# Last stage of a four-layer graph network kernel: five groups keep y and x in SBUF, six groups start together, zero rows and first fetches are issued earlier

## The chip, the cores and the metric

The kernel runs on one core of a Trainium2 chip. The metric is the time of the program on the device in microseconds (us), taken as the median of several executions. Lower is better. The engines are named as the profile names them: PE is the matrix engine (PEld its weight load), DVE the vector engine, ACT the scalar engine, POOL the GpSimd engine, SP the engine that here only issues DMAs.

## The reference, cut to what matters

There are 128 batches, each with 128 nodes of 128 features (`x`, float32) and a 128 x 128 matrix of edges (`adj`, int32). Four layers follow each other, and each has the form

```
h = relu(layernorm(x));  x = x + layer(h, adj)
```

- Layer 0 averages the neighbours by relation, adds a projection of the node itself, and applies a layer norm and a relu.
- Layer 1 takes D = |h_i - h_j| for every pair of nodes, projects it to 64 channels, and normalises each channel over all batches and pairs. A leaky relu and a second projection turn that into one score per pair. The softmax of the scores (edges only) weighs the neighbours. The weighed rows are projected, giving `y`, normalised per channel over all batches and nodes, passed through a leaky relu, and projected together with `h`.
- Layers 2 and 3 are graph attention with four heads and with one: e_ij = leaky(a_i + a_j), softmax over the edges, weighed sum of the projected rows. Layer 3 ends with an elu.

The two normalisations over all batches in layer 1 are what cut the kernel into stages: nothing behind one of them can start before every batch is through.

## The kernel before, in words

A group is four batches (`G = 4`), so there are 32 groups (`NG`). The kernel has three long stages.

**First stage.** Layer 0 of each group, and the first projection of the pair differences of each batch. The projected pairs of a batch, 2 MB, are stored in DRAM (`HP`, line 368). The orders of all engines come from `_ordered`, a list planner with written costs. It starts with a search for the largest relation number (`part`, `top`, `flag`), whose result decides a branch (line 627). In these inputs the branch that is taken only fills the DRAM array of neighbour sums with a constant (line 676, two DMAs of 1.5 MB and 6 MB). Small loads of weights (lines 197, 204, 713 to 728) stand in SP's queue around that branch, where the framework's scheduler has put them; the load of group 3's `x` and `adj` (lines 416, 417) stands behind them.

**Middle stage.** It runs over slots of one batch each. `fetch` reads half a batch of `HP` (1 MB) into one of `FETCHED = 10` buffers (line 841). ACT, DVE and PE turn the halves into scores, which are written to DRAM rows along a diagonal (line 924) and read back as a square (`u`, line 931). A chain of steps per group, spread over the slots, does the softmax, the weighing and the projections. Its `stored` step writes the group's new `x` to DRAM (line 978, array `X`) and its `y` (line 980, array `Z`), except that the last `KEPT = 8` groups keep `y` in SBUF. The step of group g falls in slot 4g + 16. The cells of the DRAM rows that the diagonal leaves free must be zero. Before the slots start, the kernel sets a tile `zero` on DVE (line 808), and writes it to both row arrays (line 811). In the program this set-up, and some small DVE and PE steps, stand ahead of the first ten fetches.

**Last stage.** Layers 2 and 3, group by group, under `tc.manual_schedule()`. `attention(g)` lists the steps of a group (loads `lz` and `lx`, mask `off`, `y`, `yl`, `po`, `x1`, then two attention layers with `mv`, `rs`, `h`, `pt`, `hT`, `pr`, `v`, `sp`, `pe`, `left`, `right`, `ps`, `e`, `w`, and at the end `ex`, `x3`, `x4`, `out`). `_planned` puts them in one order for each engine. It is a list planner with the cost written beside each step; a group may start at its due time,

```
start = max([free[engine], (n - FIRST) * period] + [done[a] + HOP for a in after])
```

so that with `FIRST = 4` and `PERIOD = 12.5` five groups are due at time zero, and one more every 12.5. Only the order is used on the chip; the times are not. Groups with `y` on chip come first. `BUFS` gives the buffers of each tile, and `ONE`, `TWO` the PSUM banks (four single, two double).

An alternative last stage (behind line 1378) runs when the scores could overflow, and is not taken here.

Of the kernel before, what the change touches and what calls it, by code (L numbers as in the profile page):

```python
# [9 lines left out]
F32 = mybir.dt.float32  # L10
# [4 lines left out]
OP = mybir.AluOpType  # L15
AX = mybir.AxisListType

P = 128
G = 4
# [9 lines left out]
KC = 8  # L29
ROW = P + 2 * KH  # L30
# [3 lines left out]
PARTS = 16  # L34
FETCHED = 10
NT = KH // KC
KEPT = 8


ONE, TWO = 4, 2  # L40
PERIOD, FIRST, HOP, LANDING = 12.5, 4, 0.2, 3.0
HOP1 = 0.4
TINY = 2.0 ** -100
BUFS = {"y": 5, "x": 11, "off": 10, "st": 7, "mv2": 4, "rs2": 3, "nb2": 3, "h": 7, "hT2": 3, "v2": 3, "wr2": 6,
        "left2": 4, "right2": 4, "e0": 2, "e1": 3, "e2": 3, "e3": 2, "sums2": 2, "o2": 2, "mv3": 2, "rs3": 2,
        "nb3": 2, "hT3": 2, "v3": 2, "wr3": 4, "left3": 2, "right3": 2, "e": 2, "sums3": 2, "o3": 2, "ex": 2}


def _bcast(src, n):
# [30 lines left out]
def _planned(groups, period, banks):  # L80

    free, done = dict.fromkeys(("SP", "Pool", "ACT", "DVE", "PE"), 0.0), {}
    left = {tag: [0.0] * n for tag, n in banks.items()}
    tag = lambda name: "2" if name[0] == "2" else "1"
    waiting = [list(steps) for steps in groups]
    plan = []
    while any(waiting):
        best = None  # L90
        for n, steps in enumerate(waiting):
            for i, (name, engine, cost, after, takes, last, work) in enumerate(steps):
                if any(a not in done for a in after):
# [75 lines left out]
def tile_gnn_stack(ctx: ExitStack, tc: tile.TileContext, a: dict, out: bass.AP):  # L169
    nc = tc.nc  # L170
    NB = a["x"].shape[0]
    NG = NB // G
# [22 lines left out]
    def load(name, shape, src, pool=const):  # L195
        t = pool.tile(shape, F32, name=name)
        nc.sync.dma_start(t, src)
        return t
# [9 lines left out]
    dr = ctx.enter_context(tc.tile_pool(name="dr", bufs=1, space=bass.MemoryType.DRAM))  # L208
# [2 lines left out]


    HP = [dr.tile([P, NT, KC * P], F32, tag=f"hp{b}", name=f"hp{b}") for b in range(NB)]
    M8 = [res.tile([P, G, P], U8, tag=f"m{g}", name=f"m{g}") for g in range(NG)]
    MV1 = res.tile([P, NG, G, 2], F32, name="MV1")
    RS1 = res.tile([P, NG, G], F32, name="RS1")
# [42 lines left out]
    with tc.tile_pool(name="c0", bufs=1) as c0, tc.tile_pool(name="p0", bufs=2) as p0, ExitStack() as ctx0:  # L259
# [33 lines left out]
        def step(name, engine, cost, after, rank, work, takes=(), gives=()):  # L293
            steps.append((name, engine, cost, after, takes, gives, rank, work))
# [237 lines left out]
        found, n_part = {}, P * P // PARTS  # L532
        flat = a["adj"].rearrange("b t s -> b (t s)").rearrange("b (c n) -> c b n", c=PARTS)
        tops = search.tile([P, 2, PARTS // 2], F32, name="tops")
        less_1 = search.tile([P, 1], F32, name="less_1")
        nc.gpsimd.memset(less_1, -1.0)
        flag = const.tile([1, 1], I32, name="flag")
# [46 lines left out]
        w1T2 = c0.tile([P, 64], F32, name="w1T2")  # L584
        both_t = c0.tile([P, 2, KC, P], F32, name="both_t")

        def both_tokens():
            turns = search.tile([P, 2, P], F32, name="turns")
            nc.vector.tensor_scalar(w1T2, w1T, 2.0, None, op0=OP.mult)
            nc.vector.tensor_copy(turns, ident[:, None, :].to_broadcast([P, 2, P]))  # L590
            ahead = turns[:, 0, 1 + KC * BY_MAX:]
            ahead = bass.AP(tensor=ahead.tensor, offset=ahead.offset,
                            ap=[list(ahead.ap[0]), [KH, 2], [1, KC], [1, P]])
            nc.vector.tensor_tensor(both_t, ahead, ident[:, None, None, :].to_broadcast([P, 2, KC, P]), OP.add)
# [17 lines left out]
        step("flag", "DVE", 0.4, ["ptop"], -99, flagged, gives=("sm",))  # L612
        step("both_t", "DVE", 2.6, ["selfb"], 99, both_tokens)
        step("fold", "Pool", 0.5, [], 99, folds)
        for g in range(AHEAD):
            chain(g, selfb)

# [156 lines left out]
    early.close()  # L774
    middle = ctx.enter_context(ExitStack())
    keep = ctx.enter_context(tc.tile_pool(name="keep", bufs=1))
    Y = {g: keep.tile([P, G, P], F32, name=f"y{g}") for g in range(NG - KEPT, NG)}
    psum = middle.enter_context(tc.tile_pool(name="psum2", bufs=1, space=bass.MemoryType.PSUM))
    banks = {"ps": 3, "pk": 2, "sm": 3}
    with tc.tile_pool(name="c1", bufs=1) as c1, tc.tile_pool(name="p1", bufs=2) as p1:  # L780

        z0 = c1.tile([P, 1], F32, name="z0")
        nc.vector.scalar_tensor_tensor(z0, bias1, 0.01, bias1, op0=OP.mult, op1=OP.max)
# [19 lines left out]
                                       add_k[:, :, 4:8], op0=OP.mult, op1=OP.add)  # L803


        slots = []
        zero = c1.tile([P, G, ROW], F32, name="zero")
        nc.vector.memset(zero, 0.0)
        for n in range(2):
            rows = dr.tile([G, P, ROW], F32, tag=f"rows{n}", name=f"rows{n}")  # L810
            nc.sync.dma_start(rows.rearrange("g i r -> i g r"), zero)
            slots.append(rows)

        sk = []
        for n in range(2):
            t = c1.tile([P, G, 1 + 2 * KH], F32, name=f"sk{n}")
# [14 lines left out]
        def now(slot, place):  # L831
            for work in jobs.pop((slot, place), ()):
                work()

        fetched, prepared, scored = [], {}, {}

        def fetch(n):

            if n < 2 * NB:
                z = p1.tile([P, NT // 2 * KC * P], F32, name="z", bufs=FETCHED)  # L840
                nc.sync.dma_start(z, HP[n // 2][:, n % 2 * NT // 2:(n % 2 + 1) * NT // 2, :]
                                  .rearrange("p a b -> p (a b)"))
                fetched.append(z)

        def products(ps, parts, j0):
            for i, (w, v) in enumerate(parts):
# [56 lines left out]
        def chain(g):  # L903

            rows = slots[g % 2]
# [27 lines left out]
            def normed():  # L933
                t["h"] = pre_norm(p1, t["x"], MV1[:, g], RS1[:, g])
                t["cap"] = p1.tile([P, G, P], F32, name="cap")
                nc.gpsimd.tensor_scalar(t["cap"], M8[g], BIG, NEG12, op0=OP.mult, op1=OP.add)
                t["x1"] = p1.tile([P, G, P], F32, name="x1", bufs=3)
                nc.gpsimd.tensor_tensor(t["x1"], t["x"], over_group(bt), OP.add)  # L938

            def folded():  # L940
# [34 lines left out]

            def stored():
                nc.vector.bn_stats(ST2[:, g, :], t["y"].rearrange("p a b -> p (a b)"))
                nc.sync.dma_start(X[g], t["x1"])
                if g not in Y:
                    nc.sync.dma_start(Z[g], t["y"])  # L980

            at(s0 - 4, "s", to_rows)
# [116 lines left out]
        with tc.manual_schedule():  # L1099
            for g in range(NG):  # L1100
                chain(g)
            brief()
            for n in range(FETCHED):
                fetch(n)
            for b in range(-1, NB + 3 * G + 1):
                slot(b)

# [12 lines left out]
    with tc.If(nc.values_load(bounded, min_val=0, max_val=1) > 0) as cmp, \  # L1120
# [10 lines left out]
        def attention(g):  # L1131
# [4 lines left out]
            def step(name, engine, cost, after, work, takes=(), last=()):  # L1136
                steps.append(((g, name), engine, cost, [(g, n) for n in after], takes, last, work))
# [15 lines left out]
            def load(name, src):  # L1153
                nc.sync.dma_start(sb(name, [P, G, P]), src)

            on_chip = g in Y
            if on_chip:
                t["y"] = Y[g]
            else:
                step("lz", "SP", 0.4, (), lambda: load("y", Z[g]))  # L1160
            step("lx", "SP", 0.4, (), lambda: load("x", X[g]))

            def masked():
                nc.gpsimd.tensor_scalar(sb("off", [P, G, P], BF16), M8[g], 0.0, None, op0=OP.is_equal)

            step("off", "Pool", 1.5, ("lx",), masked)
            step("y", "ACT", 0.75, () if on_chip else ("lz",), lambda: nc.scalar.activation(
                t["y"], t["y"], AF.Identity, bias=bias2, scale=scale2[:, 0:1]))
            step("yl", "DVE", 0.65, ("y",), lambda: nc.vector.scalar_tensor_tensor(
# [2 lines left out]
            def rest():  # L1172
                po = bank("po")
                for k in range(G):
                    nc.tensor.matmul(po[:, k, :], t["y"][:, k, :], wtyT, start=True, stop=True)

            step("po", "PE", 0.9, ("yl",), rest, takes=("po",))
            step("x1", "DVE", 0.6, ("po", "lx"), lambda: nc.vector.tensor_tensor(t["x"], t["x"], t["po"], OP.add),
                 last=("po",))

            def layer(n, heads, wx, first):
# [194 lines left out]
            return steps  # L1376

        with tc.manual_schedule():
            for work in _planned([attention(g) for g in sorted(range(NG), key=lambda g: g not in Y)], PERIOD, {"1": ONE, "2": TWO}):
                work()  # L1380


    with cmp.Else(), tc.tile_pool(name="c2", bufs=1) as c2, tc.tile_pool(name="p2", bufs=5) as p2, \
# [83 lines left out]
        def group(g):  # L1467
            zT = Y[g] if g in Y else p2.tile([P, G, P], F32, name="zT")
            if g not in Y:
                nc.sync.dma_start(zT, Z[g])  # L1470
            x = p2.tile([P, G, P], F32, name="x", bufs=6)
            nc.sync.dma_start(x, X[g])
            yT = p2.tile([P, G, P], F32, name="yT")
            nc.scalar.activation(yT, zT, AF.Identity, bias=bias2, scale=scale2[:, 0:1])
            nc.vector.scalar_tensor_tensor(yT, yT, 0.01, yT, op0=OP.mult, op1=OP.max)
# [121 lines left out]
```

## Time and profile before

| | |
|---|---|
| median of three executions | 2812.61 us (2811.74 to 2816.77) |
| the profiled execution | 2813.74 us |
| its span, first to last instruction | 2811.9 us |
| mean granted PE clock | 0.961 |
| busy: PE, DVE, ACT, POOL | 2466.4, 2472.0, 2392.2, 1723.5 us |
| first stage | to about 1528 us |
| middle stage | about 1533 to 2336 us |
| last stage | about 2336 to 2812 us |

Share of busy time is an average over three stages that have different limits, so each stage is read for itself. The rows of digits in the page give the stages at a glance: each digit is the busy tenths of one fortieth of the span, some 70 us. A row of the timeline gives the start and duration of an instruction, and in brackets the idle time of its engine before it and what ended it. SPq is the queue of DMA issues; "to landing" is the time from an issue until the data have arrived.

### The profile page before, as it was taken

Reading aid. Unit: us, or ns where it says so; the run is one execution under the profiler, and the core shown is the slowest. Engines: PE = TensorE matmul, PEld = TensorE weight load, DVE = VectorE, ACT = ScalarE, POOL = GpSimd, SP = SyncE. Lnnn points to the kernel's source line nnn. Section 1 sums busy time; section 2 is a strip of 40 time slices with the busy share of each in tenths; the row PEclk is TensorE's granted clock in tenths of the full one; section 3 lists DMA queues with packets and bytes.
Section 4 is the critical chain, followed back from the end, with each engine's and each line's share of the span. In section 5 each row is a group of like instructions: output and inputs, shape, how many; then the busy total and the mean of one; then the engine's idle time right before and its main releaser. Section 6 shows DMA issues by size and latency. Waiting matters only on the chain.

```text
span 2811.9 us, 41767 instructions
## 1 busy us (share of the span) xinstructions
PE 2466.4 (88%) x14521; PEld 1190.8 (42%) x14521; DVE 2472.0 (88%) x4713; ACT 2392.2 (85%) x2837; POOL 1723.5 (61%) x1628
## 2 busy tenths in 40 slices
PE   3899999999999999999997798998888887998897
PEld 2333333333333333333332344444444445777775
DVE  4899999999999999999997588888888886988786
ACT  4899999999999999999997787788888755988886
POOL 6799999999999999999985000111000115655552
PEclk7999999999999999999998899999999997999998
DMA  7454555455555545555546999999999961111110
GB/s 272 172 212 202 203 214 210 199 206 205 214 206 213 210 199 206 210 213 210 206 187 240 417 410 412 413 413 412 412 412 413 409 223 42 57 61 58 61 35 28
DMA packets 180379, 653.45 MB, mean 232 GB/s; under 512 B 31028, under 2 KB 98743, under 8 KB 130999
## 3 DMA queue, kind: packets, MB, share of 16 engines
q1 hardware_dynamic: 179712, 650.44, 58.5%
q8 instruction: 120, 1.97, 0.3%
q14 instruction: 109, 0.88, 0.1%
q10 hardware_dynamic: 438, 0.17, 0.0%
HBM read 337.75 MB, written 312.80 MB: 231 GB/s over the span
## 4 chain that ended last, share of the span: by engine, by line
ACT 34%; PE 25%; DVE 21%; DMA 7%; issue 7%; POOL 5%; SPq 0%; ACTq 0%; DVEq 0%; POOLq 0%
ACT d L350 14%; ACT hs L333 10%; PE hp L319 6%; PE ps L849 6%; DVE z L892 4%; DVE d L309 3%; PE hp L322 2%; PE pv L1319 2%; DMA z<-hp 2%; POOL d L309 2%; PE pk L856 2%; DMA rows<-sk 2%; ACT o L450 1%; ACT h L491 1%; ACT hn L450 1%
## 5 line engine op out<-in xcount | busy, mean ns | idle before, releaser
L309 POOL TENSOR_TENSOR d<-xe 128x2048 f32<-128x2048 f32 x256 | 1074.4, 4202 | 60.5 <-PE hp L319 55.0
L319 PE MATMUL hp<-d,w1T 128*64 128x512 f32 x4096 | 997.5, 602 | 120.3 <-ACT hs L333 84.4
L350 ACT ACTIVATE d<-d 128x2048 f32<-128x2048 f32 x384 | 734.4, 1934 | 38.5 <-DVE d L309 20.0
L309 DVE TENSOR_TENSOR d<-xe,xp 128x2048 f32<-128x2048 f32 x256 | 579.5, 2264 | 6.9 <-PE hp L319 3.5
L319 PEld LDWEIGHTS hp<-d,w1T 128*64 128x64 f32 x4096 | 285.8, 137 | 638.9 <-issue 479.2
L333 ACT COPY hs<-hp 128x1024 f32<-128x1024 f32 x512 | 516.4, 1028 | 31.1 <-PE hp L322 25.2
L938 POOL TENSOR_TENSOR x<-x,bt 128x512 f32<-128x512 f32 x32 | 44.9, 1402 | 689.3 <-DMA x<-x 626.1
L340 DVE BATCH_NORM_STATS2 st<-hs 128x6 f32<-128x512 f32 x512 | 349.3, 682 | 42.1 <-ACT hs L333 41.7
L341 DVE BATCH_NORM_STATS2 st<-hs 128x6 f32<-128x512 f32 (+1 forms) x512 | 329.3, 643 | 0.0
L892 DVE SCALAR_TENSOR_TENSOR z<-z 128x2048 f32<-128x2048 f32 x128 | 294.5, 2301 | 21.8 <-ACT z L874 21.8
L874 ACT ACTIVATE z<-z,bias,scale 128x2048 f32<-128x2048 f32 x128 | 267.2, 2088 | 18.2 <-DMA z<-hp 17.8
L878 ACT ACTIVATE zr<-z,bias,scale 128x2048 f32<-128x2048 f32 x128 | 267.3, 2088 | 9.2 <-DMA z<-hp 7.9
L322 PE MATMUL hp<-both_t,xw 128*64 128x512 f32 x1024 | 268.0, 595 | 0.0
L849 PE MATMUL ps<-z,w2z 128*32 128x512 f32 x1024 | 144.3, 636 | 79.1 <-DVE z L892 79.1
L856 PEld LDWEIGHTS pk<-pick,su 128*128 128x128 f32 x1024 | 128.0, 196 | 131.7 <-DVE su L870 85.0
L1319 PE MATMUL pv<-wr,e 128*128 128x128 f32 x1024 | 148.0, 293 | 10.7 <-DVE e L1296 6.2
L856 PE MATMUL pk<-pick,su 128*128 128x16 f32 x1024 | 140.5, 269 | 15.8 <-DVE su L870 15.8
L849 PE MATMUL ps<-z,w2l 128*32 128x512 f32 x1024 | 141.9, 624 | 0.3 <-DMA z<-hp 0.3
L1319 PEld LDWEIGHTS pv<-wr,e 128*128 128x128 f32 x1024 | 133.5, 204 | 19.3 <-issue 3.6
L849 PE MATMUL ps<-zr,w2r 128*32 128x512 f32 x1024 | 140.8, 622 | 0.4 <-ACT zr L878 0.4
L322 PEld LDWEIGHTS hp<-both_t,xw 128*64 128x64 f32 x1024 | 80.7, 138 | 141.2 <-issue 141.2
L1296 DVE SCALAR_TENSOR_TENSOR e<-e,ps 128x512 f32<-128x512 f32 x160 | 106.8, 678 | 28.7 <-ACT ps L1293 28.0
(243 smaller groups left out, 3837.4 us busy)
## 6 DMA issues: line engine op xcount, KB each, us to landing
hp<-hs SPq DMA_DIRECT2D x128, 2048.0 KB, 6.7
z<-hp SPq DMA_DIRECT2D x256, 1024.0 KB, 14.2
x<-x SPq DMA_DIRECT2D x128, 256.0 KB, 11.6
u<-rows SPq DMA_DIRECT2D x32, 384.0 KB, 11.5
x<-in_x_dram SPq DMA_DIRECT2D x32, 256.0 KB, 3.0
adj<-in_adj_dram SPq DMA_DIRECT2D x32, 256.0 KB, 3.3
part<-in_adj_dram SPq DMA_DIRECT2D x16, 512.0 KB, 7.6
out_dram<-x SPq DMA_DIRECT2D x32, 256.0 KB, 2.5
```

Source lines behind the costliest of these rows:

```text
L309: eng.tensor_tensor(d, ahead, x[:, None, None, :].to_broadcast([P, 2, KC, P]), OP.max if t == BY_MAX else OP.subtract)
L319: nc.tensor.matmul(hp[64 * hh:64 * hh + 64, c:c + 512], w1T2 if by_max else w1T, d[:, hh, c:c + 512], start=True, stop=not by_max, skip_gr ...
L322: nc.tensor.matmul(hp[64 * hh:64 * hh + 64, c:c + 512], XW[i // NT // 2][:, i // NT % 2, :], both_t.rearrange("p h k i -> p h (k i)")[:, h ...
L333: nc.scalar.copy(halves[b][:, t, :], linear.pop(i))
L340: nc.vector.bn_stats(st[:, 2 * t, :], hs[:, 0:512])
L341: nc.vector.bn_stats(st[:, 2 * t + 1, :], hs[:, 512:1024 - P * last])
L350: nc.scalar.activation(diffs[i], diffs[i], AF.Abs)
L849: nc.tensor.matmul(ps[32 * c:32 * c + 32, :], w[:, w0:w0 + 32], v[:, 512 * c:512 * c + 512], start=j0 == 0, stop=w is w2r, skip_group_chec ...
L856: nc.tensor.matmul(pk[:, kk, 0:16], su[:, kk, :], pick.rearrange("p h j -> p (h j)"), start=True, stop=True)
L878: nc.scalar.activation(zr, z1, AF.Relu, bias=bias1, scale=scale1[:, 0:1])
L892: nc.vector.scalar_tensor_tensor(z0, z0, 0.01, z0, op0=OP.mult, op1=OP.max)
L1319: nc.tensor.matmul(t[pv][:, k % 2, hd, :], t[e][:, hd, :], flat[:, at:at + P], start=True, stop=True)
```

## The change

The edits, in the order in which they take effect:

- The two row arrays are created at the top. Their zeros are written in the first stage from a tile of 128 x 192 that POOL sets, read four times over by each DMA. The step `zero` stands on SP behind the last `part`.
- The first ten fetches of the middle stage are placed ahead of its set-up, and the DVE memset and the two zero DMAs are gone from there.
- `KEPT` goes from 8 to 5, and the kept groups (27 to 31) now keep `x` in SBUF as well: `X1[g]` is written by the chain, `X[g]` is neither stored nor loaded for them. Groups 24, 25 and 26 now store `y` and load it again.
- In the last stage `FIRST` is 5 and `PERIOD` 12, and the numbers of buffers change.

```
-KEPT = 8
+KEPT = 5
...
-PERIOD, FIRST, HOP, LANDING = 12.5, 4, 0.2, 3.0
+PERIOD, FIRST, HOP, LANDING = 12, 5, 0.2, 3.0
...
-BUFS = {"y": 5, "x": 11, "off": 10, "st": 7, "mv2": 4, "rs2": 3, "nb2": 3, "h": 7, "hT2": 3, "v2": 3, "wr2": 6,
-        "left2": 4, "right2": 4, "e0": 2, "e1": 3, "e2": 3, "e3": 2, "sums2": 2, "o2": 2, "mv3": 2, "rs3": 2,
-        "nb3": 2, "hT3": 2, "v3": 2, "wr3": 4, "left3": 2, "right3": 2, "e": 2, "sums3": 2, "o3": 2, "ex": 2}
+BUFS = {"y": 6, "x": 12, "off": 10, "st": 8, "mv2": 3, "rs2": 3, "nb2": 3, "h": 7, "hT2": 3, "v2": 3, "wr2": 7,
+        "left2": 5, "right2": 5, "e0": 2, "e1": 2, "e2": 2, "e3": 2, "sums2": 3, "o2": 2, "mv3": 2, "rs3": 2,
+        "nb3": 2, "hT3": 2, "v3": 2, "wr3": 3, "left3": 2, "right3": 2, "e": 2, "sums3": 3, "o3": 3, "ex": 3}
...
+    slots = [dr.tile([G, P, ROW], F32, tag=f"rows{n}", name=f"rows{n}") for n in range(2)]
...
+        zero = search.tile([P, ROW], F32, name="zero")
+        nc.gpsimd.memset(zero, 0.0)
...
+        def no_scores():
+            for r in slots:
+                nc.sync.dma_start(r.rearrange("g i r -> i g r"), zero[:, None, :].to_broadcast([P, G, ROW]))
...
+        step("zero", "SP", 1.0, [("part", PARTS - 1)], 99, no_scores)
...
-    Y = {g: keep.tile([P, G, P], F32, name=f"y{g}") for g in range(NG - KEPT, NG)}
+    Y, X1 = ({g: keep.tile([P, G, P], F32, name=f"{n}{g}") for g in range(NG - KEPT, NG)} for n in ("y", "x1"))
...
+        fetched, prepared, scored = [], {}, {}
+
+        def fetch(n):
...
+        for n in range(FETCHED):
+            fetch(n)
...
-        slots = []
-        zero = c1.tile([P, G, ROW], F32, name="zero")
-        nc.vector.memset(zero, 0.0)
-        for n in range(2):
-            rows = dr.tile([G, P, ROW], F32, tag=f"rows{n}", name=f"rows{n}")
-            nc.sync.dma_start(rows.rearrange("g i r -> i g r"), zero)
-            slots.append(rows)
...
-                t["x1"] = p1.tile([P, G, P], F32, name="x1", bufs=3)
+                t["x1"] = X1[g] if g in Y else p1.tile([P, G, P], F32, name="x1", bufs=3)
...
-                nc.sync.dma_start(X[g], t["x1"])
                 if g not in Y:
+                    nc.sync.dma_start(X[g], t["x1"])
                     nc.sync.dma_start(Z[g], t["y"])
...
-            for n in range(FETCHED):
-                fetch(n)
...
             if on_chip:
-                t["y"] = Y[g]
+                t["y"], t["x"] = Y[g], X1[g]
             else:
                 step("lz", "SP", 0.4, (), lambda: load("y", Z[g]))
-            step("lx", "SP", 0.4, (), lambda: load("x", X[g]))
+                step("lx", "SP", 0.4, (), lambda: load("x", X[g]))
+            lx = () if on_chip else ("lx",)
...
-            step("off", "Pool", 1.5, ("lx",), masked)
+            step("off", "Pool", 1.5, lx, masked)
...
-            step("x1", "DVE", 0.6, ("po", "lx"), lambda: nc.vector.tensor_tensor(t["x"], t["x"], t["po"], OP.add),
+            step("x1", "DVE", 0.6, ("po",) + lx, lambda: nc.vector.tensor_tensor(t["x"], t["x"], t["po"], OP.add),
```

More of the change, by code (lines that the diff above doesn't have):

```diff
@@ L780, in tile_gnn_stack @@
     with tc.tile_pool(name="c1", bufs=1) as c1, tc.tile_pool(name="p1", bufs=2) as p1:
+        fetched, prepared, scored = [], {}, {}
+        def fetch(n):
+            if n < 2 * NB:
+                z = p1.tile([P, NT // 2 * KC * P], F32, name="z", bufs=FETCHED)
+                nc.sync.dma_start(z, HP[n // 2][:, n % 2 * NT // 2:(n % 2 + 1) * NT // 2, :]
+                                  .rearrange("p a b -> p (a b)"))
+                fetched.append(z)
+        for n in range(FETCHED):
+            fetch(n)
         z0 = c1.tile([P, 1], F32, name="z0")
@@ L833, in now @@
                 work()
[L835 to L843, printed above, removed]
         def products(ps, parts, j0):
@@ L1378, in tile_gnn_stack @@
         with tc.manual_schedule():
-            for work in _planned([attention(g) for g in sorted(range(NG), key=lambda g: g not in Y)], PERIOD, {"1": ONE, "2": TWO}):
+            groups = [attention(g) for g in sorted(range(NG), key=lambda g: g not in Y)]
+            for work in _planned(groups, PERIOD, {"1": ONE, "2": TWO}):
                 work()
@@ L1470, in group @@
                 nc.sync.dma_start(zT, Z[g])
-            x = p2.tile([P, G, P], F32, name="x", bufs=6)
-            nc.sync.dma_start(x, X[g])
+            x = X1[g] if g in Y else p2.tile([P, G, P], F32, name="x", bufs=6)
+            if g not in Y:
+                nc.sync.dma_start(x, X[g])
             yT = p2.tile([P, G, P], F32, name="yT")
```

## Prediction

> **What bounds the kernel now.** I read the rows of slices first, since the change touches three stages that have different limits.
>
> ```profile
> PE   3899999999999999999997798998888887998897
> DVE  4899999999999999999997588888888886988786
> POOL 6799999999999999999985000111000115655552
> DMA  7454555455555545555546999999999961111110
> ```
>
> In the first stage (slices 1 to 21) the engines are at 9 and DMA at 5: compute sets the pace. In the middle stage (23 to 32) DMA is at 9. In the last, DMA is nearly idle, and PE and DVE share the load at 8, with POOL at 5.
>
> Then the timeline, where the change acts. First the group-3 load behind the branch:
>
> ```profile
> 46.31 1.31 SPq L676 DMA_DIRECT2D a<-selfb  x2
> 64.44 6.49 SPq L727 DMA_DIRECT2D a<-in_a_dram  x4
> 71.51 0.40 SPq L416 DMA_DIRECT2D x<-in_x_dram  x1
> 74.35 0.87 DVE L427 BATCH_NORM_STATS2 lnst<-x 128x6 f32<-128x128 f32 x4 [20.56 <-DMA x<-in_x_dram]
> 77.82 1.97 PE L319 MATMUL hp<-d,w1T 128*64 128x512 f32 x4 [15.26 <-DVE d L309]
> ```
>
> Two large constant fills go out at 46.31; the second takes 22.6 us to land, at 69.67. SP's small loads wait behind it, the `x` of group 3 goes out at 71.51, and DVE stands 20.56 us for it, PE 15.26. Whatever delays that load delays everything.
>
> Second, the start of the middle stage:
>
> ```profile
> 1532.75 0.32 SPq L841 DMA_DIRECT2D z<-hp  x1
> 1536.63 0.92 SPq L811 DMA_DIRECT2D rows<-zero  x2
> 1538.10 2.09 ACT L874 ACTIVATE z<-z,bias,scale 128x2048 f32<-128x2048 f32 x1 [11.78 <-DMA z<-hp]
> 1544.74 2.09 ACT L878 ACTIVATE zr<-z,bias,scale 128x2048 f32<-128x2048 f32 x1 [4.55 <-DMA z<-hp]
> 1547.23 2.09 ACT L874 ACTIVATE z<-z,bias,scale 128x2048 f32<-128x2048 f32 x1 [0.39 <-DMA z<-hp]
> ```
>
> Only one fetch gets out at 1532.75. SP then waits for the DVE set-up and the zeros until 1537.60. Halves then arrive 2.5 us apart (1544.74, 1547.23): DMA-bound.
>
> Third, the last stage, by stretches:
>
> ```profile
> 2340.00:2370.00 30.00, 22.39 (x120) 18.09 (x121) 18.87 (x71) 17.46 (x39) 22.01 (x55) 0.75 0.16 56
> 2400.00:2500.00 100.00, 91.84 (x685) 73.70 (x686) 89.36 (x280) 91.35 (x215) 61.64 (x161) 0.98 0.21 64
> 2500.00:2650.00 150.00, 131.01 (x946) 105.11 (x945) 126.61 (x417) 125.24 (x293) 89.14 (x237) 0.94 0.19 59
> 2650.00:2750.00 100.00, 92.34 (x678) 74.63 (x678) 83.21 (x263) 86.48 (x205) 51.04 (x158) 0.96 0.14 41
> 2780.00:2812.00 32.00, 15.39 (x86) 11.91 (x84) 14.63 (x37) 10.94 (x25) 4.05 (x15) 0.63 0.13 36
> ```
>
> The columns are PE, PEld, DVE, ACT and POOL busy, granted PE clock, DMA share and GB/s. PE is fullest, at 92% in two stretches and 87% in the one between. Both ends are thin.
>
> **The change, part by part.**
>
> *Zeros moved to the first stage.* POOL's memset of 128 x 192 is about 0.2 us (its 128 x 128 one takes 0.20) and lies in a 2.51 us wait for `adj`: 0. On SP two issues (0.92 us) stand behind the last `part`, so the search's data and the flag aren't delayed; between that and the branch DMA is at 0.25 to 0.5 of its time: 0. But the scheduler puts SP's small loads differently around them. In the built order four that stood ahead of the branch (`b_2c`, `wtyT`, two of `a`) now stand behind it. There SP is held until the second fill lands; before, four small issues follow that moment ahead of group 3's `x`, now eight. SP's own arrival at the branch hardly moves (two issues more, four fewer, and `adj` of group 2 still waits for POOL near 41.6). Four issues at 0.45 us (69.69 to 71.51 is 1.82 for four) are **+1.8 us**, on the path, since DVE's statistics of group 3 wait with all pair work behind them. Low end 0 (SP reaches the branch 1.8 earlier), high end +2.5 (`adj` now comes after an `agg`, one issue more).
>
> *Fetches ahead of set-up.* The first fetch waits for the last `hp` store to land and stays at 1532.75. The second now follows it at once, so its data come 2.5 us behind the first's (1538.1): 1540.6, where 1544.74 was. That is **-4.1 us** for the whole chain of halves. At full rate the two zero writes (0.786 MB) are 1.9 us of it. The trace says more: around them DMA moved 250 to 308 GB/s, against 410 to 430 just after. From 1537.5 to 1542 about 1.29 MB took 4.5 us, where 413 GB/s needs 3.1, so they cost 3.3. [...] I take the trace. The gain lasts only while DMA, not PE at half clock in its first 15 us, sets the pace: PE's first release (about 1548 before) comes long before ten fetches (25 us) are used up.
>
> *KEPT 8 to 5.* `stored` of group g falls in slot 4g + 16, and the last fetch in slot 122 (2268.36). The three new `Z` stores (groups 24 to 26, slots 112 to 120) fall inside the DMA-bound part: 3 x 0.262 MB at 413 GB/s = **+1.9 us**. Other price: with `Z`, SP's reads of `u` recur every 23.4 us, in the groups without it 22.3, so 1.1 a group, +3.3. I take bytes, and keep both. The five `X` stores saved (slots 124 on) come after the last fetch, so they are worth 0: SP's waits of 23 us there (`x<-x` x3) hold nothing that the chain needs.
>
> *Start of the last stage.* The kept groups wait for no `x` (the second `x1` stood until 2345.41), and six groups are due at once. POOL is the limit there: 22 of 30 us. From its built order: four masks first (2340.66 + 4 x 1.56 = 2346.9), so the first root starts as before (2347.24); behind that fewer masks (1.5 to 2.0 each) stand between the roots (1.9 each) and piece sets (1.4 to 1.6). Adding these up, the third group's pieces end near 2365.3 (2367.4 before), the sixth group's root near 2368.8 (2373.1). Between -2.1 and -4.3: **-3 us**. Bounds: 0 (PE at clock 0.75 is the limit) and -7.6 (all PE idle time of the stretch).
>
> *Steady part.* Each engine does the same work, in another order. Counting in DVE's order how many groups are open when a group starts, from the ninth on: 6.8 on average before, with eight of 24 at six or fewer; 7.5 after, with four. The thin stretch 2500 to 2650 has 19.0 us of PE idle; at its neighbours' rate (15.8 in 200) it would have 11.9, so shallow flight costs about 7 us, and most of it goes: **-5 us**. This is the least certain term. No row shows the new order; bounds are half of all 34.8 idle us either way, +17 and -17.
>
> *End.* Behind the last `x2` DVE has 27 instructions in both orders, in nearly the same sequence: 0.
>
> *Buffers.* `e1` and `e2` go from 3 to 2. `e0` and `e3` have 2 already, and no row shows a wait for them. 0; its worst is in the third rival.
>
> Sum: +1.8 - 4.1 + 1.9 - 3 - 5 = -8.4. The profiled execution took 2813.74 us (span 2811.9, 1.8 around it), 1.1 above the median of 2812.61; against the median this gives **2804 us**.
>
> **The rivals.**
>
> *The last stage closes more of its holes.* If half of the 34.8 idle PE us goes, the steady term is -17 instead of -5: 2792. For it: spacing 12 is near the engines' own load (DVE 382 us in 32 groups, 11.9 each). Against: PSUM banks stay at four and two.
>
> *Only the ends move.* Order does nothing in the steady part, and each `Z` costs 1.1: +1.8 - 4.1 + 3.3 - 3 = -2: 2810.6, no change to speak of. For it: PE is at 92% already.
>
> *Slower: deeper flight meets the same four single banks.* A step `pe` must wait until an `e` of another group has freed its bank. The waits of PE on that between 2400 and 2770 are 14.7 us in nine (longest 3.3), plus 5.7 for POOL's pieces. With ten groups open, and two buffers instead of three for `e1` and `e2`, they may double: +20 in place of -5, so 2829. The other terms give -3.4, so it is slower once the steady part loses more than 3.4, and by over 0.2% from 9 on. Against it: one single bank is held a few us only, and the planner counts banks.
>
> That the zeros or fetches do not move is excluded by the built order.
>
> **How the numbers follow.** A difference of about 0.2% (5.6 us) is what a measurement of this kernel can tell from none. My sum has 0.60, the denser last stage 0.15, only the ends 0.15, deeper waits 0.10. The sum's own range, with its terms' bounds, is 2798 to 2811, and five sixths of it are faster by over 5.6 us: 0.50; with 0.15 from the dense case and 0.02 from the ends, faster is 0.67. Same is 0.09 + 0.11 = 0.20. Slower is 0.10 and 0.03 of tails: 0.13. The range 2788 to 2814 leaves out most of the slower case and the ends of the others.
>
> **What would show it.** Group 3's `x` issued near 73.3. The second half of the first batch used by ACT near 1540.6. The last stage's start 0.4 us earlier than before in all. POOL done with the sixth group's root 28 us after the first mask (32.4 before). PE idle time between 60 and 410 us after the first mask below 30. I am wrong if the last stage (first mask to end, 471.2 us before) takes more than 468 or less than 455, or if the start's gain is gone by the end of the middle stage.

## The result, and the profile after

The changed kernel takes 2800.09 us (median of four, 2799.57 to 2804.66), and the kernel before 2814.69 us beside it (2811.74 to 2818.45). The ratio is 0.9951, with a 95% interval of 0.9934 to 0.9969: 9 to 19 us, about 14. The forecast was 2804, some 8.6 us less than before. The profiled execution of the changed kernel took 2800.51 us, its span is 2798.6, its mean PE clock 0.968.

Behind the edits the lines of the code shift: L416 is now L418, L676 is L685, L727 is L736, L874 and L878 are L878 and L882. The rows of slices of the changed kernel, from the page:

```profile
PE   3899999999999999999997798888888886999986
DVE  4899999999999999999998588888888886899876
POOL 6699999999999999999986001111000115555642
DMA  7454555554555555554545999999999971121110
```

The three stages look as before; in slices 35 to 38 PE now stands at 9999 where it stood at 9988. What moved is too small for the digits, so the timeline comes next. The first lines are the load of group 3's `x` behind the branch, the others the start of the middle stage:

```profile
21.61 0.94 SPq L593 DMA_DIRECT2D rows<-zero  x2
46.57 1.30 SPq L685 DMA_DIRECT2D a<-selfb  x2
48.35 13.55 SPq L204 DMA_DIRECT2D b_2c<-in_b_dram  x1
63.24 7.44 SPq L736 DMA_DIRECT2D a<-in_a_dram  x4
73.59 0.40 SPq L418 DMA_DIRECT2D x<-in_x_dram  x1
76.50 0.87 DVE L429 BATCH_NORM_STATS2 lnst<-x 128x6 f32<-128x128 f32 x4 [23.69 <-DMA x<-in_x_dram]
...
1534.02 13.72 SPq L796 DMA_DIRECT2D z<-hp  x12
1539.22 2.09 ACT L878 ACTIVATE z<-z,bias,scale 128x2048 f32<-128x2048 f32 x1 [11.65 <-DMA z<-hp]
1541.50 2.09 ACT L882 ACTIVATE zr<-z,bias,scale 128x2048 f32<-128x2048 f32 x1 [0.19 <-DMA z<-hp]
1544.36 2.09 ACT L878 ACTIVATE z<-z,bias,scale 128x2048 f32<-128x2048 f32 x1 [0.76 <-DMA z<-hp]
```

The zeros go out at 21.61, `b_2c` now stands behind the fills, and `x` goes out at 73.59 (71.51 before). In the middle stage ACT uses the second and third half 7.48 and 10.34 us behind the first fetch, where it was 11.99 and 14.48 before.

The last stage, in the stretches that the forecast showed of before:

```profile
2340.00:2370.00 30.00, 24.69 (x155) 19.08 (x156) 23.20 (x87) 22.52 (x53) 25.78 (x60) 0.87 0.18 67
2400.00:2500.00 100.00, 91.73 (x657) 72.46 (x657) 84.77 (x266) 87.47 (x205) 57.98 (x160) 0.95 0.19 60
2500.00:2650.00 150.00, 139.35 (x1057) 111.92 (x1057) 136.16 (x446) 137.55 (x327) 95.24 (x264) 0.99 0.20 62
2650.00:2750.00 100.00, 86.27 (x633) 69.34 (x632) 80.95 (x250) 80.95 (x191) 41.39 (x132) 0.97 0.11 33
```

The thin stretch from 2500 to 2650 has filled: PE is busy 139.35 us of 150, with 1057 matmuls (131.01 and 946 before). The stretch behind it is thinner than before (86.27 against 92.34). About half of that is position, since the work runs out 13 us earlier: the 100 us that lie as far from the end as that stretch did before, 2636.7 to 2736.7, have PE busy for 89.27.

Three marks split each profiled execution: the first fetch (first `z<-hp`), the first mask of the last stage (first `off<-m` on POOL), and the end of the span.

| us | to the first fetch | to the first mask | to the end |
|---|---|---|---|
| before | 1532.75 | 807.9 | 471.2 |
| changed | 1534.02 | 806.0 | 458.6 |

So nearly all of it lies in the last stage. That stage has three parts in the diff: an order of steps (from FIRST and PERIOD), the numbers of buffers, and x on chip. The experiments take them apart.

### The profile page after: what moved, and what is told of

It is laid out like the page before. It is cut to its first block, busy times and chain, and to the rows that moved or that the text cites. A ratio compares the mean times of both kernels' runs of the same rounds, so it can differ in the third digit from the quotient of the medians.

```text
span 2798.6 us, 41745 instructions
## 1 busy us (share of the span) xinstructions
PE 2453.5 (88%) x14521; PEld 1178.8 (42%) x14521; DVE 2474.2 (88%) x4712; ACT 2391.9 (85%) x2837; POOL 1720.2 (61%) x1629
## 4 chain that ended last, share of the span: by engine, by line
ACT 35%; PE 22%; DVE 21%; DMA 8%; issue 7%; POOL 5%; SPq 0%; ACTq 0%; DVEq 0%; POOLq 0%
ACT d L352 14%; ACT hs L335 10%; PE hp L321 5%; PE ps L853 5%; DVE z L896 4%; DVE d L311 3%; DMA rows<-sk 3%; POOL d L311 3%; DMA z<-hp 2%; DMA u<-rows 2%; PE hp L324 2%; PE pk L860 2%; ACT h L1206 2%; PE pv L1322 2%; ACT h L493 1%
## 5 line engine op out<-in xcount | busy, mean ns | idle before, releaser
L878 ACT ACTIVATE z<-z,bias,scale 128x2048 f32<-128x2048 f32 x128 | 267.3, 2088 | 19.0 <-DMA z<-hp 19.0
L882 ACT ACTIVATE zr<-z,bias,scale 128x2048 f32<-128x2048 f32 x128 | 267.4, 2089 | 4.7 <-DMA z<-hp 3.8
L1322 PE MATMUL pv<-wr,e 128*128 128x128 f32 x1024 | 140.5, 283 | 5.9 <-DVE e L1299 4.0
```

The lines of the kernel that those rows point to most:

```text
L882: nc.scalar.activation(zr, z1, AF.Relu, bias=bias1, scale=scale1[:, 0:1])
L1322: nc.tensor.matmul(t[pv][:, k % 2, hd, :], t[e][:, hd, :], flat[:, at:at + P], start=True, stop=True)
```

## The experiments

Ratios are against the kernel before, timed beside each run. Theory: the order makes the gain. Rivals: transfers that are gone make it, or the buffers do.

**The old order on the changed kernel (e1).**

```
-PERIOD, FIRST, HOP, LANDING = 12, 5, 0.2, 3.0
+PERIOD, FIRST, HOP, LANDING = 12.5, 4, 0.2, 3.0
...
```

`BUFS` has its old numbers here as well.

> The changed kernel with only FIRST, PERIOD and BUFS put back (4, 12.5 and the old numbers); five groups still keep y and x on chip, zeros and fetches stay early. Stage lengths of the two kernels, from the first fetch to the first mask and from there to the end: before 807.9 and 471.2 us, changed 806.0 and 458.6. Theory (the order of the last stage, set by FIRST and PERIOD, made most of the 12.6 us): the last stage takes 468 to 471 and the time is 2809 to 2812, the rest being what the missing wait for x is worth at the start. Rival (x on chip and the loads gone made it): the last stage stays at 459 to 461 and the time at 2800 to 2803.

Measured: last stage 472.8 us, ratio 1.0018 (1.0011 to 1.0025): 5 us slower than the kernel before. The rival with x on chip is out. The other parts of the change do not carry the last stage, and the old constants do not even give the old order back, since the steps of the kept groups no longer wait for a load.

**x loaded again, order kept (e8).**

```
-                t["x1"] = X1[g] if g in Y else p1.tile([P, G, P], F32, name="x1", bufs=3)
+                t["x1"] = p1.tile([P, G, P], F32, name="x1", bufs=3)
...
+                nc.sync.dma_start(X[g], t["x1"])
...
+                step("lx", "SP", 0.4, (), lambda: nc.sync.dma_start(t["x"], X[g]))
```

> The changed kernel, with x of groups 27 to 31 stored to DRAM by the chain and loaded into the same X1 tiles at the start of the last stage, with no step of the plan told of it, so that the order of PE, DVE, ACT and POOL in the last stage is that of the changed kernel to the instruction. Theory (order): the last stage stays at 458.6 plus at most 2 us, since only the first x1 steps can meet a late x; time 2800 to 2802. Rival (transfers): most of the 12.6 us comes back, the last stage takes 466 or more, time 2807 or more. The five stores lie behind the last fetch in the middle stage and should cost nothing there by both.

Measured: ratio 0.9958 (0.9945 to 0.9971), last stage 461.5. The five stores and five loads cost nothing that shows. The 2.9 us between 461.5 and 458.6 need a look, since the order is the same. First the changed kernel, then this one, in the first 28 us behind the first mask, from the windows of each trace:

```profile
2340.01:2368.01 28.00, 22.70 (x144) 18.18 (x145) 21.28 (x77) 20.52 (x48) 24.93 (x55) 0.86 0.19 72
```

```profile
2339.17:2367.17 28.00, 23.97 (x132) 19.87 (x133) 20.51 (x75) 19.22 (x45) 23.46 (x53) 0.75 0.20 71
```

In the changed kernel's profiled execution PE was granted 0.86 of its clock there, and got 144 matmuls done in less busy time; here it was granted 0.75 and did 132. The difference goes on behind these 28 us. The whole last stage, the changed kernel first:

```profile
2340.01:2798.60 458.59, 400.91 (x2912) 319.32 (x2912) 380.87 (x1216) 381.61 (x895) 250.72 (x705) 0.95 0.16 48
```

```profile
2339.17:2800.70 461.53, 405.36 (x2912) 323.72 (x2912) 381.13 (x1216) 381.83 (x895) 251.10 (x705) 0.94 0.16 48
```

The same 2912 matmuls kept PE busy for 400.9 us there and for 405.4 here. Of six profiles with the changed kernel's order, two have 0.86 or 0.87 in the first 28 us (PE busy 400.3 and 400.9, last stage 458.6 and 459.2 us), and four have 0.74 or 0.75 (PE busy 405.4 to 407.0, last stage 461.5 to 463.0). The kernel before had 0.74, and PE was busy for 407.6. So about 3 of the 12.6 us go with the clock of that execution and not with the change; against the one profile of before, the order is worth 8 to 10.

**Zeros and fetches back in their places (e3).**

```
-        step("zero", "SP", 1.0, [("part", PARTS - 1)], 99, no_scores)
...
-        for n in range(FETCHED):
-            fetch(n)
...
+            nc.sync.dma_start(rows.rearrange("g i r -> i g r"), zero[:, None, :].to_broadcast([P, G, ROW]))
...
+            for n in range(FETCHED):
+                fetch(n)
```

> The changed kernel with the zeros of the rows and the first ten fetches back behind the set-up of the middle stage (the tile of zeros keeps its 128 x 192 form, now set by DVE). Theory (the forecast's two terms): the first fetch goes out at 1532.7 again (1534.0 in the changed kernel, so -1.3), the second half of the first batch is used by ACT 4 us later behind it, and this is still there at the first mask: 2342.8 where 2340.0 was, time +2.8, 2803. Rival (the gain at the start is eaten by the end of the middle stage): the first mask comes near 2338.7 and the time is 2799, the zeros' place being a loss alone.

Measured: ratio 0.9969 (0.9957 to 0.9981), median 2804.65, first fetch at 1533.8, first mask at 2340.9. The mask lies between the two expectations and the time beside the first one; single profiles scatter by some 2 us in either stage, and the ratio is not to be told from those of e7, e8 and e4 (0.9958 to 0.9968). The middle stage by itself is clearer. The third use of a half comes 12.98 us behind the first fetch (10.34 in the changed kernel), and the middle stage takes 807.1 us. Eleven profiles with the early fetches have 803.2 to 807.1, mean 804.8; the kernel before and two others without them (this one and e9 below) have 807.1 to 807.9, mean 807.4. The gain at the third half, 2.6 us in this kernel, is on average still there at the end of the stage, so the rival is out. It is 2.6 and not 4.1 for two reasons that the traces show. The tile of zeros is smaller here, so that DVE sets it in 0.22 us and not in 0.70; and the third half scatters, since e9, whose start is that of the kernel before, has it at 13.80 and the kernel before at 14.48. Zeros and fetches were not moved one without the other.

**One constant at a time, and the buffers alone (e5, e6, e7).**

```
-PERIOD, FIRST, HOP, LANDING = 12, 5, 0.2, 3.0
+PERIOD, FIRST, HOP, LANDING = 12, 4, 0.2, 3.0
```

> The changed kernel with FIRST 4 for 5 and nothing else edited: five groups are due at time zero, spacing stays 12, buffers stay. The last stage of the changed kernel took 458.6, 459.2 and 462.3 us in three profiles with the same order; with FIRST, PERIOD and BUFS all old it took 472.8. Theory (the six groups due at once are the start, worth about 3, and the spacing of 12 the steady part): the last stage takes 462 to 465, time 2802 to 2805. Rival (one group more at a time is what fills PE all the way through, spacing is secondary): 468 or more, time 2808 or more.

```
+PERIOD, FIRST, HOP, LANDING = 12.5, 5, 0.2, 3.0
```

> The changed kernel with PERIOD 12.5 for 12 and nothing else edited. At 12.5 the group of number n is due (n - 5) x 0.5 us later, 13 us for the last. Theory (spacing makes the steady part's gain): the last stage takes 467 to 472, time 2807 to 2812. Rival (the number of groups in flight, FIRST, makes it): 459 to 463, time 2800 to 2803.

```
-BUFS = {"y": 6, "x": 12, "off": 10, "st": 8, "mv2": 3, "rs2": 3, "nb2": 3, "h": 7, "hT2": 3, "v2": 3, "wr2": 7,
...
+BUFS = {"y": 5, "x": 11, "off": 10, "st": 7, "mv2": 4, "rs2": 3, "nb2": 3, "h": 7, "hT2": 3, "v2": 3, "wr2": 6,
...
```

> The changed kernel with the old numbers of buffers and the new FIRST and PERIOD, so that the order of every engine in the last stage is the changed kernel's to the instruction; only waits for a free buffer can differ. Theory (the forecast costed the buffers at nothing, and the gain is the order's): the last stage stays at 459 to 462, time 2800 to 2803. Rival (the denser order needs its buffers: five left2 and right2, seven wr2, eight st, twelve x): 464 or more, time 2805 or more.

Measured: FIRST 4 gives 1.0028 (1.0017 to 1.0038) and a last stage of 478.8 us, the slowest of all; PERIOD 12.5 gives 1.0002 (0.9993 to 1.0010) and 474.8; the old buffers give 0.9968 (0.9958 to 0.9979) and 463.0. Against e8 and e4, whose intervals overlap with that, the buffers are worth 0 to 3 us. The two constants were both expected to give part of the gain, and both runs were slower than that allows (465 and 472): with one of them alone on the changed kernel nothing is left of it.

The thin stretch, 160 to 310 us behind the first mask, shows it. From the windows of the kernel before, of e5 and of e6:

```profile
2500.66:2650.66 150.00, 131.01 (x943) 105.05 (x942) 126.61 (x415) 125.24 (x293) 89.72 (x239) 0.94 0.20 60
```

```profile
2498.87:2648.87 150.00, 129.94 (x937) 102.24 (x936) 123.60 (x390) 126.55 (x296) 82.64 (x230) 0.95 0.18 57
```

```profile
2497.11:2647.11 150.00, 134.01 (x978) 105.78 (x978) 129.05 (x415) 130.53 (x304) 85.80 (x233) 0.97 0.20 59
```

On the changed kernel, of these settings only 5 and 12 together bring PE to 139.35. Whether a hole opens in the middle is decided by how the whole order falls, not by one setting.

**FIRST 5 alone, on the kernel before (e9).** The function that builds the order ends with a time of its own, in the costs written beside its steps. It is no time of the chip, but it was there to be tried.

```
-PERIOD, FIRST, HOP, LANDING = 12.5, 4, 0.2, 3.0
+PERIOD, FIRST, HOP, LANDING = 12.5, 5, 0.2, 3.0
```

> The kernel before with FIRST 5 for 4 and nothing else edited: PERIOD stays 12.5, eight groups keep y only, x is loaded, zeros and fetches stay late. So far neither new constant alone was worth anything on the changed kernel: its last stage took 472.8 us with FIRST 4 and PERIOD 12.5, 478.8 with 4 and 12, 474.8 with 5 and 12.5, and 458.6 to 463.0 with 5 and 12. The step function of the kernel that builds the order has an end time of its own, in the costs written beside its steps (not a time of the chip): 447.3, 452.5, 443.2 and 437.1 for these four, and 443.0 for the kernel before (471.2 measured). Theory (what counts is how well the one order that comes out happens to fit, and the planner's own end tells it): for this kernel that end is 437.7, so the last stage takes 461 to 465 and the time is 2801 to 2806, without x on chip and without PERIOD 12. Rival (FIRST 5 pays only together with PERIOD 12, or only with x on chip): 470 to 475, 2811 to 2816.

Measured: last stage 461.6 us, ratio 0.9972 (0.9961 to 0.9982). This is what the planner's end promised. One digit, with x loaded, eight groups of y and the old spacing and buffers, gives the last stage's gain: the ratio is that of e3 (0.9969), which has the changed last stage and late fetches as well. In this one profile 3.9 of the 9.6 us are PE's idle time, and the rest is PE's busy time (401.9 us where before it was 407.6), at a mean granted clock of 0.95 in that stage against 0.93. Its stretch from 160 to 310 us:

```profile
2501.57:2651.57 150.00, 138.82 (x1033) 109.75 (x1032) 132.85 (x434) 134.21 (x318) 90.92 (x253) 0.99 0.20 59
```

**PERIOD 12.3 (e10).**

```
-PERIOD, FIRST, HOP, LANDING = 12, 5, 0.2, 3.0
+PERIOD, FIRST, HOP, LANDING = 12.3, 5, 0.2, 3.0
```

> The changed kernel with PERIOD 12.3 for 12 and nothing else edited. Theory (the planner's own end tells the order's worth): that end is 432.9 where the changed kernel has 437.1, so the last stage takes 454 to 459 us where the changed kernel has about 462, and the time is 2794 to 2798. Rival (spacing has a smooth effect, and 12.3 lies between 12 at 462 and 12.5 at 475): the last stage takes 468 to 472, time 2807 to 2811.

Measured: ratio 0.9945 (0.9932 to 0.9958), last stage 460.5. The smooth effect of spacing is out: 12 and 12.3 are good, 12.5 is not. The time, 2797.13, is in the expected range, the last stage is not (454 to 459). Two more kernels with 12.3 (below) have 457.4 and 460.6, and the mean of the three, 459.5, stands against 462.3 for the four profiles of the order with 12 at the lower clock. That is some 3 us, too few for the timed runs to tell from nothing.

All orders side by side, with PE's idle time in the last stage (its length less PE's busy time):

| order (FIRST, PERIOD) | planner's own end | PE idle, us | last stage, us |
|---|---|---|---|
| 5, 12.3 (e10, e12, e13) | 432.9 | 54.7 to 56.3 | 457.4 to 460.6 |
| 5, 12 (changed; e3, e4, e7, e8, e11) | 437.1 | 56.0 to 58.9 | 458.6 to 463.0 |
| 5, 12.5 on before (e9) | 437.7 | 59.8 | 461.6 |
| 4, 12.5 (before) | 443.0 | 63.7 | 471.2 |
| 5, 12.5 (e6) | 443.2 | 63.8 | 474.8 |
| 4, 12.5 (e1) | 447.3 | 65.9 | 472.8 |
| 4, 12 (e5) | 452.5 | 71.1 | 478.8 |

The planner's end parts the good orders from the bad ones. By length it does not rank e6 and e1, but by PE's idle time it ranks all of them, up to the overlap of the first two. The rest of the length is PE's busy time, which was 400.3 to 410.9 us for the same 2912 matmuls; the most is e6's, at the lowest granted clock (0.92). Two of these orders (e9, e10) were expected from the planner's end before they ran; for the others it was compared afterwards.

**The wait for group 3's x (e4, e11, e12, e13).** The change delayed this load. Can the whole stall go?

```
-                nc.sync.dma_start(t.rearrange("p n g t -> p n (g t)"),
+                nc.scalar.dma_start(t.rearrange("p n g t -> p n (g t)"),
```

> The changed kernel with the two large constant fills behind the branch issued from ACT's DMA queue instead of SP's; nothing else is edited. In the changed kernel SP's small loads stand behind the fills and group 3's x goes out at 73.6; DVE then stands 23.7 us for it and PE 18.2. Theory (it is a queue that is full, not the memory, that holds the loads, and the stall is on the path): x of group 3 goes out near 55, the stall of DVE falls below 8 us, the first fetch comes at 1534.0 less 12 to 18, and all of it reaches the end: 2782 to 2788. Rival (bandwidth: the fills take the DMA engines whoever issues them): x is issued early but lands no sooner than 8 us before it did, first stage -5 to -8, 2792 to 2795. Second rival (the stages behind are not moved): 2800.

Measured: ratio 0.9960 (0.9947 to 0.9972), `x` issued at 72.93. None of the three mechanisms fits: 2800 is the time that the last one named, but `x` is issued as late as before. From the timeline of SP, and the waits of SP's queue from 44 to 76 us:

```profile
47.60 0.33 SPq L204 DMA_DIRECT2D b_2c<-in_b_dram  x1
...
49.12 20.89 SPq L736 DMA_DIRECT2D a<-in_a_dram  x4
```

```profile
SPq L736 <- DMA a<-selfb: 18.5, 2, 16.5
```

With the fills in another queue `b_2c` goes out in 0.33 us, so the first 13.55 us were indeed the queue. But now one of the small loads stands 16.5 us for the fill to land. It needs nothing from it, and the fill is in the other queue. Why it waits for that fill was not tried by itself.

Next the fills on POOL's queue, and the ten loads of `a_2` and `a_3` behind the first stage (e11). The two edits were not tried apart.

```
+                nc.gpsimd.dma_start(t.rearrange("p n g t -> p n (g t)"),
...
+            for work in _ordered(steps, {"sm": 2}, HOP1):
+                work()
             for part in range(2):
...
-            for work in _ordered(steps, {"sm": 2}, HOP1):
-                work()
```

> The changed kernel with the two constant fills behind the branch issued from POOL's DMA queue, and the ten small loads of a_2 and a_3 issued after all work of the first stage instead of ahead of it. With the fills on ACT's queue nothing was gained: x of group 3 still went out at 72.9, because one of the small loads stood 16.5 us for the 6 MB fill. [...] Theory (this wait, and not bandwidth or a full queue, is the whole stall): x of group 3 goes out near 50, its statistics start near 54 instead of 76.5, the first fetch comes 15 to 20 us earlier (1514 to 1519), and the time is 2781 to 2786. Rival (bandwidth): x goes out near 50 but lands only at 65 to 72 behind the fill, time 2790 to 2797. Second rival (POOL needs time of its own to issue 3840 rows, and its masks come late): the gain is eaten, 2798 to 2805.

```profile
49.15 1.36 SPq L418 DMA_DIRECT2D x<-in_x_dram  x1
...
63.25 0.87 DVE L429 BATCH_NORM_STATS2 lnst<-x 128x6 f32<-128x128 f32 x4 [8.30 <-DMA x<-in_x_dram]
```

Measured: ratio 0.9934 (0.9920 to 0.9947), median 2792.79, first fetch at 1520.8. `x` goes out 24.4 us earlier, but DVE can use it only 14.1 us later, where 2.9 were enough in the changed kernel after the fill had landed. That is the rival's case and its time (2790 to 2797): part of the stall was the wait, and part is left beside the fill. From 48 to 69 us, which covers those 14.1, the DMA engines are busy nine tenths or more of every slice, and 7.86 of the 9.04 MB moved from 45 to 75 us go through the fills' queue. DVE's start and the first fetch are both some 13 us earlier; the timed runs show about 7 of it against e8 and e4. No loss from POOL's issuing shows.

With AHEAD 3 the load stands ahead of the branch (e12, with PERIOD 12.3):

```
-AHEAD = 2
+AHEAD = 3
```

> The changed kernel with PERIOD 12.3, the fills on POOL's queue, the loads of a_2 and a_3 behind the first stage, and AHEAD 3 for 2, so that group 3's x is loaded ahead of the branch and the fills. With the fills on POOL's queue and the loads moved, x of group 3 was issued at 49.2 and used at 63.3 (76.5 in the changed kernel), because it still shared the DMA engines with the fills. Theory: with the load ahead of the branch the rest of that stall, about 8 us of DVE, goes too; the first fetch comes near 1512 to 1516, and with 12.3 the last stage takes 454 to 459; time 2775 to 2783. Rival (ahead of the branch the fourth group's work delays the flag, or the next group's load meets the fills instead): first fetch at 1518 to 1524, time 2783 to 2790.

Measured: ratio 0.9947 (0.9934 to 0.9960), first fetch at 1536.0. A miss, and for the reason that the rival named, but by more than it allowed. The load was early, but one more group's layer 0 now stands ahead of the branch, and PE stands idle 18.10 us for its first step. The fills behind the branch go out at 69.74, and at 45.86 in e11; the first `hp` matmul starts at 76.84, and at 50.66 in the changed kernel. From the timelines of PE and POOL:

```profile
48.66 1.63 PE L462 MATMUL pt<-ident,hn 128*128 128x128 f32 x4 [18.10 <-ACT hn L452]
...
69.74 2.44 POOL L685 DMA_DIRECT2D a<-selfb  x2 [1.25 <-issue]
```

The last run is e11 with PERIOD 12.3:

> The changed kernel with PERIOD 12.3, the fills on POOL's queue and the loads of a_2 and a_3 behind the first stage; AHEAD stays 2, since with 3 the first fetch came at 1536.0 and not at 1520.8. If the two gains add (the fills' and loads' 0.9934 of the time before, and 12.3's 0.9945 where the changed kernel's order gave 0.9951 to 0.9960): first fetch near 1521, last stage 457 to 461 us, time 2787 to 2792. Rival (12.3 is no better than 12, its earlier gain being scatter): 2791 to 2795.

Measured: ratio 0.9912 (0.9899 to 0.9926), median 2787.68: 12 us less than the changed kernel's, and faster than both kernels. In its profile the first fetch is at 1524.1 (1521 was expected) and the last stage takes 460.6 (457 to 461). The interval just overlaps that of e11, so the share of 12.3 is not settled.

## Why the prediction was right, and where it was not

The sum was -8.4, and about -14 with an interval of -9 to -19 came. The two runs that share the changed kernel's order and whose edits cost nothing that shows (e8, e4) have 0.9958 and 0.9960, which is -11 to -12. By stages: the first shows nothing that can be told from scatter (forecast +1.8); the middle one shows -2.8, the mean of the eleven profiles against that of before and e9 (forecast -2.2); the last one shows -8 to -10 at the lower clock (forecast -8).

- **Zeros moved, +1.8.** `x` of group 3 was issued at 73.59, forecast near 73.3. At the first fetch the profile has +1.3. But e9, whose first stage is the old one, has its first fetch at 1534.35, 1.6 later than the kernel before. So the later issue is shown, and what is left of it 1460 us later is not. That the load is on the path is shown by e11, where its use and the first fetch both come some 13 us earlier.
- **Why SP is held.** The forecast said that SP is held until the second fill lands. True, but e4 shows two holds in a row: the place behind the fills in SP's queue (13.55 us at `b_2c` in the changed kernel, 0.33 in e4), and a small load's wait for the 6 MB fill to land (16.5 us in e4). With the fills in ACT's queue only the first is gone.
- **Fetches ahead, -4.1.** ACT used the second half at 1541.50 (forecast near 1540.6). The second and third use of a half came 4.5 and 4.1 us earlier behind the first fetch, or 3.9 and 3.5 against e9, whose start is the old one too. Right, and the size taken from the trace (DMA at 250 to 308 GB/s around the zeros, so that they cost 3.3 us) fits better than -2.7, the estimate that follows with the zeros at the 413 GB/s of the halves (1.9 us). PE was not at half clock for all of its first 15 us, as the forecast has it: before, it was granted 0.50 from 1530 to 1546, 0.93 from 1546 to 1550 and 0.51 from 1550 to 1560. Nothing hung on that.
- **Three new Z stores, +1.9.** SP's reads of `u` were 2.06 us earlier than before at 2183.17 and 0.26 earlier at 2277.47: +1.8 over those groups. All profiles with the new stores take 93.6 to 94.7 us from that read of `u` to the fourth behind it, before and e9 without them 92.5 and 92.1. Right, and the other price, +3.3, is out.
- **Start of the last stage, -3.** The first mask came 0.65 us earlier than before (forecast 0.4). The third group's pieces ended 23.3 us behind the first mask, and the sixth group's root 26.9; 24.6 and 28 were forecast, and in the profiles at the lower clock (e3, e8) they came at 24.6 and 28.3. PE's idle time in the first 60 us went from 9.0 to 6.4, and is 5.1 in e7 and e8. With FIRST 4 it is 9.1 (e1, e5), though x is on chip there, and with FIRST 5 and x loaded 7.4 (e9): most of this is FIRST, and the missing wait for `x` shows nothing. That POOL is the limit does not follow from its 22.0 busy us of 30; PE had 22.4.
- **Steady part, -5, and end, 0.** The size is right. The last stage in three parts: the first 60 us, the middle, and the last 61.24; the kernel before first, then e8:

```profile
2340.66:2400.66 60.00, 51.02 (x331) 40.38 (x331) 42.45 (x151) 44.83 (x105) 39.99 (x102) 0.88 0.07 25
2400.66:2750.66 350.00, 315.25 (x2307) 253.69 (x2307) 299.21 (x957) 303.07 (x713) 201.25 (x554) 0.96 0.18 55
2750.66:2811.90 61.24, 41.29 (x277) 31.22 (x275) 40.04 (x111) 34.81 (x81) 14.78 (x50) 0.81 0.10 28
```

```profile
2339.17:2399.17 60.00, 54.88 (x367) 44.59 (x367) 48.18 (x173) 50.95 (x120) 44.98 (x113) 0.88 0.10 34
2399.17:2739.46 340.29, 310.79 (x2283) 248.61 (x2282) 293.80 (x937) 295.57 (x696) 192.67 (x545) 0.96 0.18 54
2739.46:2800.70 61.24, 39.70 (x266) 30.52 (x265) 39.15 (x108) 35.31 (x80) 13.45 (x49) 0.86 0.10 28
```

PE's idle time in the middle went from 34.8 to 29.5, and at the end from 20.0 to 21.5, where the forecast had no change. The thin stretch lost 8.3 of its 19.0 idle us (forecast were 7), but some of that came back in other stretches.
- **The reason given for it,** a deeper flight, is not shown. The forecast counted open groups: 6.8 before, 7.5 after (7.6 in the trace). Counted in the same way, e5 and e6 have 7.25, and five starts of 24 at six or fewer against eight, and neither has less PE idle time than the kernel before. So more open groups alone do not fill the hole. But the idea is not out either: the good orders all have 7.6 or more (e9 7.7, e10 7.75), the bad ones 7.25 or less.
- **PE idle from 60 to 410 us below 30.** It was 32.7. The end of this sign lies at a fixed distance from the mask, and the changed kernel has less work left there; up to 61.24 us before the end, as in the kernel before, it is 29.6.
- **Last stage between 455 and 468.** 458.6, of which about 3 are the clock of that execution.
- **The slower rival** had PE's waits for `e` double. The waits of PE from 60 to 410 us behind the first mask, before and after:

```profile
PE pe L1264 <- DVE e L1296: 13.8, 8, 3.3
PE pe L1264 <- POOL pieces L1257: 5.7, 4, 3.4
```

```profile
PE pe L1267 <- DVE e L1299: 4.3, 4, 2.3
PE pe L1267 <- POOL pieces L1260: 3.5, 3, 2.0
```

They fell to 4.3 and 3.5. But the direction was less safe than the text made it: one digit in FIRST turns the same change into +8 us (e5), and there `pe` waits only 2.4 us for `e`; other waits take the place. Buffers at 0 hold to within 3 us (e7). The reason given for the steady part would have held for e5 and e6 too, so it is in part luck that the pair 5 and 12 is one of the good ones.

Open: which property of an order makes the hole. The planner's end tells it without saying why. No single wait carries it in e1, e5 and e6, and an order with single steps swapped was not tried.

## What to carry to other kernels

When constants feed a list planner, the thing to judge is the order that comes out. Neighbouring constants moved this stage by 16 to 20 us, so each candidate has to be built and compared as a whole, first by the planner's own end, which costs nothing and here ranked PE's idle time, and then on the chip. A gain that a diff seems to owe to data kept on chip may belong to one digit beside it: put each back alone before you believe it.

## What the hardware showed beyond what was expected

- A load of 128 B in SP's queue stood 16.5 us for a 6 MB fill in ACT's queue, from which it needs nothing (e4).
- Beside a fill that POOL issued, a load of 256 KB took 14.1 us from issue to use (e11); behind the fill it took 2.9 (changed kernel).
- The clock that PE is granted at the start of a stage differs between profiles of one order (0.74 or 0.86 in 28 us), and goes with about 3 us of 460. What makes the two kinds of profile was not tried.
